# Mamba block in a four-layer graph network: the engines' order written out, one slot per state

## The chip, the cores and the metric

The kernel runs on one core of a Trainium2 chip. The metric is the device time in microseconds of one execution; the median of three runs of the kernel before is 3628.54 us (3626.14 to 3638.55). A core has five engines that each take their instructions strictly in the order in which they were built: TensorE (PE, with its weight loads as PEld), VectorE (DVE), ScalarE (ACT), GpSimd (POOL) and SyncE (SP), which here only issues DMAs. An instruction that must wait holds back everything behind it on its engine.

## The reference

There are 3327 nodes with 256 features and a 3327 x 3327 weighted adjacency. Four layers follow each other, each of the form `x = layernorm(x + layer(x, adj))`. The change touches layer 1, a graph convolution followed by a Mamba block (float32):

```python
h = relu(adj @ x @ gcn_w + gcn_b); h = layernorm(h) * ln_g + ln_b
xz = h @ w_in; xc, z = xz[:, :512], xz[:, 512:]
u = silu(causal_conv4(xc) + conv_b)
dbc = u @ w_xp                           # 16 step-size ranks, 16 of B, 16 of C
dt = softplus(dbc[:, :16] @ w_dt + b_dt)
dA = exp(dt[:, :, None] * A);  dBu = dt * B * u
hst = dA_t * hst + dBu_t;  ys_t = hst @ C_t      # scan over the 3327 rows
y = (ys + u * D_skip) * silu(z);  out = y @ w_out
```

The scan runs along the nodes, for each of 512 channels and each of 16 states.

## The kernel before

The nodes are padded to 26 tiles of 128. Layer 0 comes first, then the Mamba stage, then the graph attention of layer 2 and the two-step attention of layer 3. Work is traced in the text through a scheduling layer, which builds each engine's order and the semaphores from the data flow; the order of the text is a priority, not a rule. `issue_after` and `keep_in_program_order` fix an instruction behind another one of its engine.

In the Mamba stage the nodes lie along the free axis, in chunks of at most four tiles (512 columns), and the 512 channels lie on the partitions in four groups (NG = 4). The chunks have 2, 2, 3, 4, 4, 4, 4, 3 tiles. For each chunk the loop runs over 16 states; (chunk, state) is one step of the main loop, called a slot in this document. A slot has

- four decays on ACT (`decay`, L255 by its helper): `dA = exp(dt * A)` into one of two PSUM tiles;
- a feed on POOL (`feed`, L498): `h = du * B`, for the slot two later, into one of two tiles `h`;
- four scans on DVE (`scan`, L259 by its helper), each over one channel group, with the last column of the chunk before as its start (`carry`, copied by ACT in L587);
- the product with C on DVE (`product`, into one of two tiles `hc`), which the PE transposes and adds up into PSUM tiles `y`, one per node tile (`add_up`, L519).

Around this recurrence lies work that is spread over the slots. `convolve` is a generator of the graph convolution for one tile after the other (26 matmuls of 128x256 in groups of JM = 6, L278; a copy `m`, two transposes, a copy, the product with `gcn_w`, a Relu; then `measure`, `norm` and `turn`, which are statistics on DVE and POOL, a normalization on ACT and two transposes into `hT`). `pace` advances it so that it stays ahead of the chunks. `head(c + 1)` prepares the next chunk from slot 3 of chunk c, one step a slot: four input projections with the convolution's taps (to slot 8), Silu, the product with `w_xp` (slot 9), two step sizes in slot 10 and two in slot 11 (L437 to L440 on PE and ACT, then L445 on ACT), the subtraction of the softplus on DVE and Ln on ACT in slot 12, and the rest in slots 13 and 14. `gate_input` computes z in slots 2 to 5, and its Silu is in slot 8 of the text. `back(c - 1)` finishes the chunk before: gate, transposes and the output projection with the residual in slot 0, the normalization in slot 4. `values` is layer 2's value computation for finished tiles, two steps a slot once the convolution is done.

Two chains fix part of the order: `chained` queues scans, products, taps and the head's DVE steps in the order of the text, and `decaying` does so for the decays, the Silu calls and Ln on ACT. The rest of each engine's order is the scheduler's choice.

PSUM has eight banks: four `y`, two `dA`, one `cb` for the convolution, and one `ps` that projections, step sizes, `turn`, `gate_input`, `back` and `values` all share.

Of the kernel before, what the change touches and what calls it, by code (L numbers as in the profile page):

```python
# [9 lines left out]
F32 = mybir.dt.float32  # L10
# [15 lines left out]
NS = 6  # L26
# [19 lines left out]
def gnn_kernel(ctx: ExitStack, tc: tile.TileContext, n: int, a: dict, out: bass.AP):  # L46
# [109 lines left out]
    with tc.tile_pool(name="l1b", bufs=1) as wpool, tc.tile_pool(name="l1at", bufs=2) as l1at:  # L156
# [33 lines left out]
        with tc.tile_pool(name="l1aw", bufs=1) as cwork, tc.tile_pool(name="l1c", bufs=2) as ch, \  # L190
                tc.tile_pool(name="l1t", bufs=3) as tmp, tc.tile_pool(name="l1s", bufs=2) as work, \
# [53 lines left out]
            while not ends or ends[-1] < npad:  # L245
                prev = ends[-1] if ends else 0
                ends.append(min(npad, prev + min(WC, max(2, len(ends) + 1) * P)))
# [3 lines left out]
            chain, decays = [], []  # L251

            def decaying(*x, **k):
                with tc.issue_after(decays[-1].ins) if decays else nullcontext():
                    decays.append(nc.scalar.activation(*x, **k))  # L255

            def chained(op, *x, **k):
                with tc.issue_after(chain[-1].ins) if chain else nullcontext():
                    chain.append(op(*x, **k))  # L259

            def power(rs, var):

                nc.gpsimd.tensor_scalar(rs, var, EPS, None, op0=ALU.add)
                nc.gpsimd.tensor_tensor(rs, rs, mhalf[:, :var.shape[1]], op=ALU.pow)

            def convolve():
# [3 lines left out]
                for it in range(nt):  # L270
                    cb = cpsum.tile([P, 2, D], F32, name="cb")
                    acc, tp = cb[:, 0, :], cb[:, 1, :]
                    for j in range(nt):
# [4 lines left out]
                        nc.tensor.matmul(acc, at[:, j % JC, :], X0[:, j, :], start=(j == 0), stop=(j == nt - 1))  # L278
# [5 lines left out]
                    nc.scalar.copy(m, acc)  # L284
# [5 lines left out]
                    for k in range(2):  # L290
                        nc.tensor.transpose(tp[:, k * P:(k + 1) * P], m[:, k * P:(k + 1) * P], ident)
                    mt = cwork.tile([P, D], F32, name="m")
                    nc.scalar.copy(mt, tp)
                    for k in range(2):
                        nc.tensor.matmul(acc, mt[:, k * P:(k + 1) * P], gw[:, k, :], start=(k == 0), stop=False)
                    nc.tensor.matmul(acc, one, gb, start=False, stop=True)
                    h = cwork.tile([P, D], F32, name="hn")
                    nc.scalar.activation(h, acc, AF.Relu)  # L298
# [4 lines left out]
                    def measure(h=h, rs=rs, nb=nb):  # L303
                        mv = small.tile([P, 2], F32, name="mv")
                        stats(mv, h)
                        power(rs, mv[:, 1:2])
                        nc.gpsimd.tensor_scalar(nb, mv[:, 0:1], rs, -1.0, op0=ALU.mult, op1=ALU.mult)

                    def norm(h=h, rs=rs, nb=nb):
                        tc.keep_in_program_order(nc.scalar.activation(h, h, AF.Identity, scale=rs, bias=nb))  # L310

                    def turn(it=it, h=h):
                        c = next(x for x in range(nch) if it * P < ends[x])
                        i = it * P - starts[c]
                        if i == 0:
                            hTs[c] = ch.tile([P, D // P, WC], F32, name="hT")
                        pt = psum.tile([P, WC], F32, name="ps")
                        for k in range(2):
                            nc.tensor.transpose(pt[:, k * P:(k + 1) * P], h[:, k * P:(k + 1) * P], ident)
                        for k in range(2):  # L320
                            nc.scalar.activation(hTs[c][:, k, i:i + P], pt[:, k * P:(k + 1) * P], AF.Identity,
                                                 scale=g1[:, k:k + 1], bias=b1[:, k:k + 1])
                    rest = [lambda: None, measure, lambda: None, norm, turn]
# [4 lines left out]
                for step in rest:  # L328
# [21 lines left out]
            def pace(c, s):  # L350


                c, s = divmod(c * DS + s + DS - 3, DS)
                t0 = ends[c] if c < nch else npad
                t1 = ends[c + 1] if c + 1 < nch else npad + P
                target = NS * (t0 + (t1 - t0) * (s + 1) / DS) / P + NS - 1
                while taken < target:
                    if not advance():
                        for _ in range(2):
                            values()  # L360
                        return

            def value(it):

                pt = psum.tile([P, WC], F32, name="ps")
                for k in range(2):
                    nc.tensor.transpose(pt[:, k * P:(k + 1) * P], X[:, it, k * P:(k + 1) * P], ident)
                xt = cwork.tile([P, D], F32, name="m")
                nc.scalar.copy(xt, pt[:, :D])
                yield  # L370
                po = psum.tile([P, WC], F32, name="ps")
                for k in range(2):
                    nc.tensor.matmul(po[:, :D + 2], xt[:, k * P:(k + 1) * P], wg[:, k, :], start=(k == 0), stop=(k == 1))
                nc.scalar.copy(col[:, it, :], po[:, D:D + 2])
                g = F[:, it, D:]
                nc.scalar.activation(g, col[:, it, 0:1], AF.Exp, scale=0.2)
                nc.scalar.mul(F[:, it, :D], po[:, :D], g)
# [12 lines left out]
            def project(c, g, w):  # L390
                ps = psum.tile([P, WC], F32, name="ps")
                for k in range(2):
                    nc.tensor.matmul(ps[:, :w], w_in[:, k, g * P:(g + 1) * P], hTs[c][:, k, :w],
                                     start=(k == 0), stop=(k == 1))
                return ps[:, :w]

            def head(c):

                w = ends[c] - starts[c]
                xc = scratch()
                nc.gpsimd.tensor_copy(xc[:, :, :3], last)
                u = us[c] = ch.tile([P, NG, WC], F32, name="u", bufs=1)[:, :, :w]
                for g in range(NG + 2):
                    if g < NG:
                        nc.scalar.copy(xc[:, g, 3:3 + w], project(c, g, w))
# [1028 lines left out]
```

## Time and profile before

| what | value |
|---|---|
| median of three runs | 3628.54 us (3626.14 to 3638.55) |
| the profiled execution | 3631.34 us, its span 3629.5 us |
| mean granted clock | 0.957 |
| PE, DVE, ACT, POOL busy over the span | 3275.3, 2412.7, 1709.0, 937.9 us |
| first scan to last product of the Mamba stage | 442.2 to 1473.3 us |
| a scan of 512 columns | 1264 ns, 256 of them |
| a product of 2048 columns | 2288 ns, 64 of them |
| a decay of 512 columns | 689 ns, 256 of them |
| a feed of 2048 columns | 4530 ns, 64 of them |
| an ACT table load | 1283 ns, 32 in the stage |

The profile is one execution taken by the hardware profiler. Busy time is the time in which an engine executed; the idle time ahead of an instruction is put down to what released it. A line of the form `DVE t L259 <- ACT t L445: 39.8, 6, 12.4` says that DVE's instruction that writes tile `t` in line 259 waited for ACT's instruction that writes `t` in line 445, 39.8 us in all, 6 times, 12.4 us at most. In a timeline, a row gives start, length, engine, line, operation, output and inputs, and in brackets the idle time ahead of it. Durations of neighbouring instructions on DVE and ACT overlap by some tens of ns, so a run of four is shorter than four times one. Because operations go through helpers, scans, products and taps share L259 and are told apart by their tiles.

### The profile page before, as it was taken

To read this page: it belongs to the slowest core of one execution; us is meant where nothing else is said; L and a number is where in the kernel's file an instruction comes from. 1 tells how busy PE (TensorE), PEld (TensorE's weight loads), DVE (VectorE), ACT (ScalarE), POOL (GpSimd) and SP (SyncE) were. 2 spreads that over 40 slices of the span, in tenths; PEclk is the share of its full clock that TensorE was granted. 3 is DMA by queue.
4 is the path that set the end of the run, shared out by engine and by line. 5 is a ranking of instruction groups with operands and counts; after the bars stand their busy time and mean duration, and the time that the engine had idled before them with its cause. 6 is when DMAs were issued, how large, how long until landed. Compare 5 with 4: busy or idle time off the path is not lost. (4 is left out here: it accounts for less than half of the span.)

```text
span 3629.5 us, 43459 instructions
## 1 busy us (share of the span) xinstructions
PE 3275.3 (90%) x15583; PEld 2562.6 (71%) x15583; DVE 2412.7 (66%) x5460; ACT 1709.0 (47%) x2642; POOL 937.9 (26%) x967
## 2 busy tenths in 40 slices
PE   9999988888788666699979999999999899999996
PEld 7888666666665445588858777787777667777775
DVE  1111287888989988677753445445451999999996
ACT  1000466556555565211133333333335888888883
POOL 0000154555555545111110000000000233333332
PEclk9999999998999888799989999999999999999998
DMA  7443334333333222244422121121222122222220
GB/s 249 135 140 99 104 100 108 102 95 110 96 103 88 60 53 57 90 138 147 147 63 63 47 66 56 54 65 51 60 63 64 47 62 63 68 68 68 68 60 19
DMA packets 151996, 308.01 MB, mean 85 GB/s; under 512 B 19858, under 2 KB 77394, under 8 KB 151634
## 3 DMA queue, kind: packets, MB, share of 16 engines
q1 hardware_dynamic: 151762, 305.06, 28.4%
q8 instruction: 126, 2.06, 0.2%
q14 instruction: 108, 0.88, 0.1%
HBM read 294.36 MB, written 10.65 MB: 84 GB/s over the span
## 5 line engine op out<-in xcount | busy, mean ns | idle before, releaser
L498 POOL TENSOR_TENSOR h<-du,row 128x2048 f32<-128x2048 f32 (+2 forms) x128 | 475.6, 3716 | 411.4 <-DVE hc L259 310.3
L259 DVE TENSOR_TENSOR_SCAN h<-dA,carry,h 128x512 f32<-128x512 f32 (+2 forms) x448 | 478.8, 1113 | 54.3 <-ACT dA L255 51.3
L255 ACT ACTIVATE dA<-dt,A_log 128x512 f32<-128x512 f32 (+2 forms) x512 | 309.0, 609 | 232.0 <-DVE h L259 228.0
L912 PE MATMUL acc<-X,wt 128*128 128x256 f32 x1352 | 345.2, 392 | 10.5 <-ACT wt L910 10.2
L879 PE MATMUL acc<-F,at 128*128 128x256 f32 x1352 | 352.4, 386 | 1.0 <-ACT q L653 0.6
L278 PE MATMUL cb<-F,at 128*128 128x256 f32 x1352 | 333.6, 397 | 12.2 <-ACT hn L298 12.1
L912 PE MATMUL acc<-G,wt 128*128 128x256 f32 x1352 | 336.0, 391 | 4.4 <-ACT wt L843 4.0
L519 PE MATMUL y<-ident,hc 128*128 128x128 f32 x1664 | 249.4, 302 | 77.7 <-DVE hc L259 77.4
L912 PEld LDWEIGHTS acc<-X,wt 128*128 128x128 f32 x1352 | 243.7, 190 | 105.7 <-issue 41.3
L118 PE MATMUL acc<-xa,at 128*128 128x257 f32 x1352 | 308.4, 381 | 6.0 <-DMA at<-in_adjT 6.0
L278 PEld LDWEIGHTS cb<-F,at 128*128 128x128 f32 x1352 | 263.6, 200 | 69.2 <-ACT hn L298 18.2
L519 PEld LDWEIGHTS y<-ident,hc 128*128 128x128 f32 x1664 | 217.2, 157 | 130.9 <-DVE hc L259 100.0
L879 PE MATMUL acc<-X,at 128*128 128x256 f32 x1352 | 308.4, 381 | 0.0
L788 PE MATMUL acc<-F,at 128*128 128x257 f32 x1352 | 304.5, 381 | 1.7 <-DMA U<-in_U 1.7
L912 PEld LDWEIGHTS acc<-G,wt 128*128 128x128 f32 x1352 | 249.9, 192 | 63.9 <-ACT wt L843 33.8
L924 DVE MAX8 cand<-e 128x8 f32<-128x128 f32 x676 | 142.2, 279 | 227.7 <-ACT e L865 216.2
L879 PEld LDWEIGHTS acc<-F,at 128*128 128x128 f32 x1352 | 237.1, 190 | 74.9 <-issue 50.2
L118 PEld LDWEIGHTS acc<-xa,at 128*128 128x128 f32 x1352 | 255.2, 190 | 43.2 <-issue 6.7
L879 PEld LDWEIGHTS acc<-X,at 128*128 128x128 f32 x1352 | 252.9, 191 | 39.8 <-issue 6.6
L788 PEld LDWEIGHTS acc<-F,at 128*128 128x128 f32 x1352 | 254.1, 191 | 37.6 <-issue 1.9
L259 DVE TENSOR_TENSOR hc<-h,row 128x2048 f32<-128x2048 f32 (+2 forms) x128 | 246.5, 1926 | 4.7
L910 ACT COPY wt<-tp 128x512 f32<-128x512 f32 (+1 forms) x182 | 93.8, 557 | 310.8 <-PE tp L908 310.3
(302 smaller groups left out, 5180.3 us busy)
## 6 DMA issues: line engine op xcount, KB each, us to landing
at<-in_adjT SPq DMA_DIRECT2D x102, 832.0 KB, 4.5
at<-in_adjT SPq DMA_DIRECT2D x260, 320.0 KB, 3.0
row<-bc SPq DMA_DIRECT2D x64, 512.0 KB, 4.9
at<-in_adjT SPq DMA_DIRECT2D x52, 576.0 KB, 4.1
at<-in_adjT SPq DMA_DIRECT2D x26, 512.0 KB, 3.7
row<-bc SPq DMA_DIRECT2D x32, 384.0 KB, 4.8
row<-bc SPq DMA_DIRECT2D x32, 256.0 KB, 4.6
xt<-in_xT SPq DMA_DIRECT2D x26, 128.0 KB, 4.1
```

Source lines behind the costliest of these rows:

```text
L118: nc.tensor.matmul(acc, at[:, j, :], rhs[:, j0 + j, :], start=(j0 + j == 0), stop=(j0 + j == nt - 1))
L255: decays.append(nc.scalar.activation(*x, **k))
L259: chain.append(op(*x, **k))
L278: nc.tensor.matmul(acc, at[:, j % JC, :], X0[:, j, :], start=(j == 0), stop=(j == nt - 1))
L498: nc.gpsimd.tensor_tensor(hs[k % 2][:, :, :w], du, rows[k][:, 0:1, :].to_broadcast([P, NG, w]), op=ALU.mult)
L519: nc.tensor.matmul(y[:, g * P:(g + 1) * P], h[:, g, i * P:(i + 1) * P], ident, is_transpose=True, start=(first and g == 0), stop=(last and ...
L788: nc.tensor.matmul(acc, at[:, j, :], F[:, j0 + j, :], start=(j0 + j == 0), stop=(j0 + j == nt - 1))
L879: nc.tensor.matmul(acc, at[:, j, :], rhs[:, j0 + j, :], start=(j0 + j == 0), stop=(j0 + j == nt - 1))
L910: copy(wt[:, :m, :], pt[:, :m, :])
L912: nc.tensor.matmul(acc, wt[:, j, :], rhs[:, j0 + j, :], start=(j0 + j == 0), stop=(j0 + j == nt - 1))
L924: nc.vector.max(cand[:, s * 8:(s + 1) * 8], z[:, s * SEG:(s + 1) * SEG])
```

## The change

In the main loop of the Mamba stage every instruction on PE, DVE, ACT and POOL is now pinned behind the one traced before it on its engine (`Ordered`, `pinned`), so each engine's order is the order of the text; DMAs stay free. The text is written in slots:

- A slot begins with the `add_up` of the slot before, then four scans with the decays, the carry, the product and the feed.
- The next chunk's head is a class `Head` with one method for each step, called in fixed slots: projections in 5 and 6, taps in 7 to 9, Silu in 9 (with that of z), `mixed` in 10, step sizes in 10, 11, 11 and 12, the exponentials in 12, the subtraction and Ln in 13, `finish` in 14, `skip` in 15. The four Exp and the four Identity of 128x512 become one each of 128x2048. The step size stays in the scratch tile.
- The chunk before is finished tile by tile: gates in slot 0 between the scans, transposes and projection of one tile in each of slots 1 to 4, its residual add on DVE in the slot after, its statistics one slot later, the scales in slot 6, the normalization in 7 and 8. z is computed in 7 and 8.
- `uses` are a slot's pieces that go through `ps`; the convolution's steps (`work_ahead`, in number by `quota`) are put between and behind them. The convolution has one more yield a tile (NS = 7), and its lead begins at slot 5 (S0).
- `value` goes through the bank `cb` instead of `ps`; the scratch pool has four buffers instead of three, and `hT` three instead of two.
- The chunks have 2, 2, 3, 3, 4, 4, 4, 4 tiles.

```diff
-NS = 6
+NS = 7
+S0 = 5
...
-                ends.append(min(npad, prev + min(WC, max(2, len(ends) + 1) * P)))
+                ends.append(min(npad, prev + min(WC, (2 + len(ends) // 2) * P)))
...
+                def __getattr__(self, name):
+                    op = getattr(self.engine, name)
+                    if not pinned:
+                        return op
+                    return lambda *x, **k: tc.keep_in_program_order(op(*x, **k))
+            ten, vec, act, gps = (Ordered(x) for x in (nc.tensor, nc.vector, nc.scalar, nc.gpsimd))
...
-                    rest = [lambda: None, measure, lambda: None, norm, turn]
+                    rest = [lambda: None, measure, lambda: None, lambda: None, norm, turn]
...
-                pt = psum.tile([P, WC], F32, name="ps")
+                pt = cpsum.tile([P, WC], F32, name="cb")
...
+                def step_size(self, g):
+                    w = self.w
+                    if g == 0:
+                        self.v, self.e = (scratch()[:, :, :w] for _ in range(2))
+                    ps = psum.tile([P, WC], F32, name="ps")
+                    k = slice(32 * g, 32 * g + DTR)
+                    ten.matmul(ps[:, :w], w_dt[k, :P], self.left[k], start=True, stop=True)
+                    act.activation(self.v[:, g, :], ps[:, :w], AF.Identity, bias=b_dt[:, g:g + 1])
+                    act.activation(self.e[:, g, :], ps[:, :w], AF.Abs, bias=b_dt[:, g:g + 1])
+                def exponentials(self):
+                    e = self.e
+                    act.activation(e, e, AF.Exp, scale=-1.0)
+                    self.e1 = scratch()[:, :, :self.w]
+                    act.activation(self.e1, e, AF.Identity, bias=1.0)
+                def logarithms(self):
+                    vec.scalar_tensor_tensor(self.e, self.e1, 1.0, self.e, op0=ALU.subtract, op1=ALU.subtract)
+                    act.activation(self.e1, self.e1, AF.Ln)
...
+                if added:
+                    add_up(*added)
                 for g in range(NG):
                     scan(k, g, dAs.pop(0))
...
+                    if c and s == 0:
+                        for i in range(tiles_of(c - 1)):
+                            if min(i + 1, NG - 1) == g:
+                                gate(c - 1, i)
+                    if g == 0 and s - 1 in sums:
+                        sums.pop(s - 1)()
+                    if g == 1 and c and 2 <= s < 2 + tiles_of(c - 1):
+                        measured(plus["mv"][:, s - 2, :], X[:, starts[c - 1] // P + s - 2, :])
+                act.copy(carry[:, s, :], hs[k % 2][:, :, w - 1])
...
+                if s == 9:
+                    act.activation(szs[c], szs[c], AF.Silu)
+                if after:
+                    for g in {7: (0, 1), 8: (2,), 9: (3,)}.get(s, ()):
+                        ahead.taps(g)
+                    if s == 9:
+                        ahead.silu()
+                    elif s == 13:
+                        ahead.logarithms()
+                    elif s == 14:
+                        ahead.finish()
+                added = ys[c], product(k), False, s == DS - 1
...
+                if after:
+                    if s in (5, 6):
+                        if s == S0:
+                            pump(ends[c + 1] // P)
+                        uses += [lambda g=g: ahead.project(g) for g in (2 * s - 10, 2 * s - 9)]
+                    if s == 10:
+                        uses += [ahead.mixed]
+                    uses += [lambda g=g: ahead.step_size(g) for g in {10: (0,), 11: (1, 2), 12: (3,)}.get(s, ())]
+                    if s == 12:
+                        uses += [ahead.exponentials]
+                    if s == 15:
+                        uses += [ahead.skip]
...
+                q = quota(c, s) if done < nt else 2
+                for use in uses[:1]:
+                    use()
+                work_ahead((q + 1) // 2)
+                for use in uses[1:]:
+                    use()
+                work_ahead(q // 2)
```

## The prediction

> **What bounds the kernel now.** I read the page's busy shares first, then the busy time by stage, then VectorE's waits in the stage that the diff touches, then its timeline in one chunk. Over the whole span PE is busiest, but the edit is confined to the Mamba stage, from 440 to 1475 us, so that stage is read alone. The columns are length, then busy us (instructions) of PE, PEld, DVE, ACT, POOL, then clock, DMA share and GB/s.
>
> ```profile
> span 3629.5 us, 43459 instructions
> 440.00:1475.00 1035.00, 807.75 (x3837) 601.43 (x3836) 895.96 (x889) 611.26 (x1196) 552.78 (x235) 0.90 0.33 88
> ```
>
> DVE is busy 896 of 1035 us, more than PE (808), so DVE bounds the stage and its idle time is what an order can win. VectorE's waits from 438 to 1475 us (total, times, longest):
>
> ```profile
> DVE h L259 <- ACT dA L255: 55.9, 43, 4.2
> DVE t L259 <- ACT t L445: 39.8, 6, 12.4
> DVE bnst L86 <- ACT hn L298: 25.6, 6, 10.6
> DVE u L259 <- ACT u L408: 3.1, 2, 1.7
> ```
>
> With four small ones (2.6, 2.5, 1.4, 0.9) this is 131.8 us, the most that a perfect order could save. I laid the waits on the 128 states (a "slot": four scans and a product) by the products' times. Slot 12 of each chunk holds 63 us (4.6, 11.0, 14.1, 10.0, 12.6, 3.3, 6.8, 0.2 in chunks 0 to 7), slot 9 holds 23, all others 46. Chunk 4 shows both kinds, an undisturbed slot and slot 12 (DVE's timeline, then ACT's beside it):
>
> ```profile
> 1010.20 4.80 DVE L259 TENSOR_TENSOR_SCAN h<-dA,carry,h 128x512 f32<-128x512 f32 x4
> 1015.09 2.29 DVE L259 TENSOR_TENSOR hc<-h,row 128x2048 f32<-128x2048 f32 x1
> 1017.30 4.80 DVE L259 TENSOR_TENSOR_SCAN h<-dA,carry,h 128x512 f32<-128x512 f32 x4
> ...
> 1041.89 2.29 DVE L259 SCALAR_TENSOR_TENSOR t<-t 128x2048 f32<-128x2048 f32 x1 [12.41 <-ACT t L445]
> ```
> ```profile
> 1026.34 0.67 ACT L438 ACTIVATE t<-ps,b_dt 128x512 f32<-128x512 f32 x1
> 1026.91 0.68 ACT L439 ACTIVATE t<-ps,b_dt 128x512 f32<-128x512 f32 x1
> ...
> 1029.75 0.69 ACT L438 ACTIVATE t<-ps,b_dt 128x512 f32<-128x512 f32 x1 [1.03 <-PE ps L437]
> ...
> 1040.20 1.66 ACT L445 ACTIVATE t<-t 128x512 f32<-128x512 f32 x3
> 1041.76 0.38 ACT L298 ACTIVATE hn<-cb 128x256 f32<-128x256 f32 x1
> 1042.15 1.28 ACT L255 ACT_TABLE_LOAD   x1
> ```
>
> A full slot takes 7.1 us (1010.20 to 1017.30). In slot 12, DVE stands before the subtraction of the softplus until ACT has worked off 14 us of step-size work, which comes one slot before its consumer.
>
> **The change part by part.** No engine gains work worth a term: the built programs differ by 48 ACT instructions fewer (and three tiny POOL ones more), and after the Mamba block the order on all five engines is the same. What moves is the order in the block.
>
> *Slot 12.* The head starts at slot 5 instead of 3, its step sizes lie in slots 10, 11, 11, 12, the joined exponentials in 12, the subtraction in 13. What is late next is found from ACT's room. Counted from the start of a full slot, the fourth scan ends at 4.8; a decay (0.6) and the carry (0.2) follow, so other ACT work starts at 5.6 and must end by 8.8, for the third decay (0.7) to be there at 7.1 + 2.4 = 9.5. That is room for 3.2 us. Slot 10 has the 112-row copy and one pair, 0.5 + 1.2: it fits. Slot 11 has two pairs with a PE round trip between (1.2 + 0.9 + 1.2), then a conv tile's copy, norm and two turned copies (0.3 + 0.5 + 0.7), which again wait for PE: about 2.2 over. Slot 12 has a pair and two 2048-wide activations (1.2 + 0.3 + 1.9 + 1.9): 2.1 over. Slot 13 has a table load, Ln and a load (1.28 + 1.9 + 1.28) after the subtraction, against 4.8 less a decay: 1.0 over. So 5.3 a head at full width; the narrow heads' shorter slots take most of what their shorter work gives, and I take 4.5 for seven heads, 31 us. Saved: 63 - 31 = 32.
>
> *Slot 9.* Both Silu calls stay there (load 1.28, 1.9, 1.9, load 1.28, with a Relu 0.4 between), now with one tap group (2.2) before the product, so 6.7 against 3.2 + 2.2: 1.3 over at full width, some 2 on the narrow slots. Eight chunks at 1.6 are 13. Saved: 23 - 13 = 10.
>
> *The other slots.* The skip product with a conv tile's copies (slot 15) is 1.3 over. A finished tile of the chunk before is now projected a slot at a time, and DVE adds it after the next slot's first scan. If the conv's turn stands before it in PE's fixed order, that add waits some 2 us, which is new. With the two projection slots I take 4.5 a chunk, 36 in all, against 46. Saved: 10.
>
> *PE's fixed order.* PE goes through one PSUM tile `ps` for nearly all helpers, and a second use in a slot must wait until ACT has copied the first (about 6 us into the slot). Behind the waiting matmul stand the conv steps and the next slot's transposes; product k waits for the transposes of k-2, so a slot of lateness is covered, but ACT's copies wait for PE, and the decays stand behind them. No row shows this wait in a fixed order. From below it is nothing, as PE has 227 us of idle time here; from above, 1.0 us a slot, as long as the round trip in the row at 1029.75, 128 us. I take 10, near the low end, because that round trip comes at most twice a slot and usually inside ACT's room; both ends go to the range.
>
> The Trainium skill, in "Perfetto Trace Analysis", Identifying the Most-Contended Engine, says that matmul busy time misjudges PE and the weight loads' share should be read instead; here that is 601 of 1035 us (58%) against 78%. By that share the term would be nearer 0; the sum keeps 10.
>
> *Joined activations.* Four Exp and four Identity of 512 become one each: three pieces took 1.66, so four take 2.2, and one of 2048 elements 1.9. That is 0.6 a head on ACT, inside the slot-12 figure. The skill's section Optimizing Scalar/DVE Operations, on the same page, says that breaking instructions up may help where ACT is not saturated but makes bubbles elsewhere, which speaks against joining. If a joined call held a decay back by its extra 1.4 us, eight heads would lose 2 x 1.4 x 8 = 22 us; the rows leave these calls in slot 12 behind both early decays in either form, so I book no such loss.
>
> *Chunks 2, 2, 3, 3, 4, 4, 4, 4.* The same widths in another order, so DVE's sum is unchanged. In PE's built order, the conv tiles done beside chunks 1 and 2 fall from 3.8 and 4.4 to 3.0 and 4.0, so the lead stays covered (7.0 tiles after chunk 0, 7.5 before). The tail has four tiles to finish rather than three: a tile's period is 3.9 us (1479.78 to 1483.68). The value step now uses the bank `cb`, which lets it lie beside the residuals (before, the third residual came 7.3 after the second). I take +2, between 0 and +4.
>
> *The first head.* Before, from 420 to 433.5 us ACT mixed conv work into the first step sizes; now four pairs, one Exp and one Identity follow each other, some 10.5 us instead of 13.5: -3, between 0 and -5.
>
> *The rest.* Row and adjacency DMAs are the same in number and on the same SP queue; the B/C rows are written in slot 10 and first read in slot 14, four slots (28 us) against a landing time of 4.9. The feeds on POOL still follow the product and take 4.5 of 7.1 us. The fourth scratch buffer and the step size in place cost nothing.
>
> The waits become 31 + 13 + 36 + 10 = 90 instead of 131.8, so -42; with +2 and -3 the sum is -43. The profiled execution took 3631.3 us (its span 3629.5), 2.8 above the median of the runs; -43 from the median, 3628.5, gives 3585.5, and I say 3586.
>
> **The rivals.**
> *A: ping-pong on `ps` and `cb` decides (slower).* Place: the second use in a slot and the copies behind it on ACT, ahead of the decays. For it: PE is 78% busy, the slots of 256 columns last only 3.7 us, and a round trip (1 us) does not shrink with them. Against: 227 us of PE idle. It decides from 0.33 us a slot more than I booked (43/128); at the upper end, 128 instead of 10, the time is 3628.5 - 43 + 118 = 3704; at half of that excess, 3645.
> *B: the stalls only move.* The 42 us that went from slots 9 and 12 come back in slots 4, 11 and 15. For it: ACT is full in those slots by the sum above. Time: 3628 - 1, about 3627.
> *C: nearly all waits go.* If PE's lateness is nothing and the overruns of slots 11 to 13 are hidden by DVE's own extra work (some 24 us a full chunk beyond its 16 slots of 7.1), the 13 and 36 remain: 3628.5 - 83 - 1 = 3545.
> *D: the change does nothing*, since each engine already ran a fixed order: excluded as such, as the orders differ throughout the block.
>
> **How the numbers follow.** Mine 0.50, C 0.17, B 0.12, A 0.21. The range reaches from just above C's figure to just below A's half: 3550 to 3640, with about a tenth left out at each end; my case alone runs from 3560 (PE's term nothing, half of the overruns hidden) to 3612 (PE's term 36). About 0.3% (11 us) is what a measurement tells from no change. Faster is mine and C with a hundredth of B, 0.68. Within it are 0.10 of B and 0.02 of A, 0.12. Slower is the rest, 0.20.
>
> **What would show it.** Right: the wait of `t` on the joined Identity falls from 40 us to under 10, DVE's waits in the block to 70 to 110, no slot is above 16 us, and DVE's busy time stays near 896. Wrong: a new wait of the X add on `ps`, or of `dA` behind copies in every slot, above 60 us together; a block longer than 1035 us; or PE waiting for ACT in most slots.

## The result, and the profile after

The changed kernel takes 3740.84 us (median of 4 runs, 3739.81 to 3741.57) against 3630.73 us before (median of 4, 3626.14 to 3638.55): a ratio of 1.0301 with a 95% interval of 1.0282 to 1.0320, 110 us slower. The forecast was 3586, its range 3550 to 3640: wrong in sign and outside the range. Of the experiments below, pin_pe and pin_pool each had one run in a slower state, which is left out of their figures.

The span of the profiled execution, and the busy time in the Mamba stage of the kernel after (columns as in the view by stage shown for the kernel before):

```profile
span 3739.6 us, 43358 instructions
433.00:1590.00 1157.00, 852.84 (x3853) 654.07 (x3853) 900.54 (x886) 606.64 (x1150) 519.71 (x239) 0.84 0.29 79
```

DVE is as busy as before (901 us, 896 before), but the stage is longer: from the first scan to the last product it takes 1156.5 us (433.3 to 1589.8), 125 more than the 1031.1 before. Around it 13 us are gained: the first scan comes 9 us earlier, and from the last product to layer 2's first `w` 28.3 us pass instead of 32.6. So the loss is idle time of DVE in the block. Laid on the slots by the products' times it is 247.9 us, against 130.8 before (each with 2.5 us ahead of the first scan):

| slot | 0 | 1 | 2 | 3 | 4 | 5 | 6 | 7 | 8 | 9 | 10 | 11 | 12 | 13 | 14 | 15 |
|---|---|---|---|---|---|---|---|---|---|---|---|---|---|---|---|---|
| before, us | 2.7 | 0 | 0 | 4.7 | 13.5 | 7.4 | 2.2 | 0.5 | 1.4 | 22.9 | 0.5 | 2.5 | 62.6 | 5.5 | 3.8 | 0.6 |
| after, us | 9.0 | 5.8 | 12.5 | 17.9 | 14.3 | 2.0 | 35.6 | 31.0 | 11.4 | 7.0 | 19.7 | 28.9 | 23.3 | 17.1 | 12.4 | 0 |

The peak of slot 12 is gone, and nearly every other slot has a wait. To read the second row: most of what the text puts into a slot on PE and ACT stands behind that slot's product, so its lateness shows at the third scan of the next slot. The projections written in slots 5 and 6 show in columns 6 and 7, the Silu calls of slot 9 in column 10, the steps from `mixed` to Ln (slots 10 to 13) in columns 11 to 14. The last chunk, which prepares no head, has no wait at all in columns 6, 7 and 11 to 14.

VectorE's waits and ScalarE's waits of the kernel after in this stage (total, times, longest):

```profile
DVE h L263 <- ACT dA L263: 201.0, 74, 7.2
DVE X L263 <- PE ps L263: 28.4, 18, 3.4
```
```profile
ACT t L263 <- PE ps L263: 87.1, 41, 5.1
ACT col L263 <- PE cb L263: 40.0, 19, 4.4
...
ACT u L263 <- POOL t L263: 31.4, 7, 5.9
```

DVE waits for decays 201 us (55.9 before) and no longer for the softplus (39.8 before). ScalarE is no busier than before (607 us, 611 before); what it gained is waiting: all its waits for PE in the stage add up to 225 us, against 94 before.

The timeline of the kernel after in chunk 4, slots 5 and 6, ScalarE first, then GpSimd, TensorE and VectorE, shows two ways in which this reaches DVE:

```profile
991.23 0.58 ACT L263 COPY t<-ps 128x512 f32<-128x512 f32 x1
997.66 0.81 ACT L263 ACTIVATE u<-t,conv_b,conv_w 128x512 f32<-128x512 f32 x1 [5.86 <-POOL t L263]
...
999.97 1.28 ACT L263 ACTIVATE dA<-t,A_log 128x512 f32<-128x512 f32 x2
...
1006.84 0.59 ACT L263 COPY t<-ps 128x512 f32<-128x512 f32 x1 [2.86 <-PE ps L263]
...
1011.16 0.58 ACT L263 COPY t<-ps 128x512 f32<-128x512 f32 x1 [2.88 <-PE ps L263]
1011.78 0.81 ACT L263 ACTIVATE u<-t,conv_b,conv_w 128x512 f32<-128x512 f32 x1
1012.50 1.28 ACT L263 ACTIVATE dA<-t,A_log 128x512 f32<-128x512 f32 x2
```
```profile
992.99 4.50 POOL L263 TENSOR_TENSOR h<-du,row 128x2048 f32<-128x2048 f32 x1 [2.58 <-DVE hc L263]
997.43 0.20 POOL L263 COPY t<-last 128x12 f32<-128x12 f32 x1
```
```profile
1004.92 1.88 PE L263 MATMUL ps<-hT,w_in 128*128 128x512 f32 x4
1006.64 2.76 PE L263 MATMUL cb<-F,at 128*128 128x256 f32 x12
1009.24 1.88 PE L263 MATMUL ps<-hT,w_in 128*128 128x512 f32 x4
```
```profile
1000.68 2.46 DVE L263 TENSOR_TENSOR_SCAN h<-dA,carry,h 128x512 f32<-128x512 f32 x2 [5.45 <-ACT dA L263]
...
1013.20 2.46 DVE L263 TENSOR_TENSOR_SCAN h<-dA,carry,h 128x512 f32<-128x512 f32 x2 [4.77 <-ACT dA L263]
```

In slot 5 ScalarE's convolution `u` needs the three halo columns that GpSimd copies; the copy takes 0.20 us but stands behind a feed of 4.5 us, and the third and fourth decay of the next slot stand behind `u`. In slot 6 ScalarE waits at two copies for the projections, between which PE has twelve convolution matmuls, and again the decays stand behind. Slot 10 of the same chunk shows the second way where little work is written: the copy of `mixed` and the first pair of step sizes take 1.85 us together, but wait 8.1 us for PE, and VectorE waits 6.1 us (ScalarE, then VectorE):

```profile
1053.30 0.58 ACT L263 COPY t<-ps 112x512 f32<-112x512 f32 x1 [5.01 <-PE ps L263]
1056.95 1.27 ACT L263 ACTIVATE t<-ps,b_dt 128x512 f32<-128x512 f32 x2 [3.06 <-PE ps L263]
1058.10 1.30 ACT L263 ACTIVATE dA<-t,A_log 128x512 f32<-128x512 f32 x2
```
```profile
1058.83 2.46 DVE L263 TENSOR_TENSOR_SCAN h<-dA,carry,h 128x512 f32<-128x512 f32 x2 [6.09 <-ACT dA L263]
```

### The profile page after: what moved, and what is told of

It reads as the page before. It is cut to its first block, busy times and chain, and to the rows that moved or that the text cites. A ratio compares the mean times of both kernels' runs of the same rounds, so it can differ in the third digit from the quotient of the medians.

```text
span 3739.6 us, 43358 instructions
## 1 busy us (share of the span) xinstructions
PE 3301.6 (88%) x15583; PEld 2604.1 (70%) x15583; DVE 2418.5 (65%) x5460; ACT 1705.0 (46%) x2594; POOL 903.5 (24%) x970
## 5 line engine op out<-in xcount | busy, mean ns | idle before, releaser
L263 ACT ACTIVATE dA<-t,A_log 128x512 f32<-128x512 f32 (+2 forms) x510 | 305.3, 609 | 276.8 <-DVE h L263 274.3
L263 PE MATMUL cb<-F,at 128*128 128x256 f32 x1148 | 296.4, 411 | 69.4 <-ACT hn L263 69.1
L263 PEld LDWEIGHTS cb<-F,at 128*128 128x128 f32 x1148 | 232.3, 207 | 133.0 <-ACT hn L263 77.2
L263 PEld LDWEIGHTS y<-ident,hc 128*128 128x128 f32 x1648 | 231.4, 166 | 110.1 <-DVE hc L263 97.1
L995 PE MATMUL tp<-ident,e 128*128 128x128 f32 x1352 | 196.6, 277 | 43.1 <-DVE e L1182 35.1
```

The lines of the kernel that those rows point to most:

```text
L263: return lambda *x, **k: tc.keep_in_program_order(op(*x, **k))
L995: nc.tensor.transpose(pt[:, j, :], e[:, (j0 + j) * P:(j0 + j + 1) * P], ident)
```

## The experiments

All kernels here compute the whole reference. Each ratio is against runs of the kernel before on the same chip, each time a median of at least 4 runs.

### Two waits inside the written order

**halo_early**: the kernel after, with the halo's copy ahead of slot 5's feed on GpSimd.

```diff
+                def halo(self):
+                    self.xc = scratch()
+                    gps.tensor_copy(self.xc[:, :, :3], last)
...
+                if s == S0 and after:
+                    ahead.halo()
                 added = ys[c], product(k), False, s == DS - 1
```

> Part done differently: in slot 5 the three-column halo copy on POOL (0.2 us) is put ahead of that slot's feed (4.5 us) instead of behind it. Theory H (the POOL order costs by itself): ACT's wait for POOL in the projections, 31.4 us in 7 waits, goes, and with it DVE's idle time at slot 6, 35.6 us; time 3741 - 31 to 36, about 3707. Rival P (PE's fixed order stands ready to take its place: the convolution waits for the same Relu and the second projection comes late anyway): under 10 us are won, 3731 or more.

Measured: 3711.83 us, ratio 1.0218 (1.0199 to 1.0237), 29 us less than the kernel after. DVE's idle time in the block falls by 31 to 217.1 us, in slot 6 from 35.6 to 14.4 and in slot 7 from 31.0 to 21. ScalarE's waits for GpSimd fall from 35 to 4 us. So the halo explains 29 us, and not more, in the pinned kernel.

**uses_first**: the kernel after, with all pieces on `ps` of a slot ahead of the convolution's steps.

```diff
-                for use in uses[:1]:
+                for use in uses:
                     use()
-                work_ahead((q + 1) // 2)
-                for use in uses[1:]:
-                    use()
-                work_ahead(q // 2)
+                work_ahead(q)
```

> Part done differently: a slot's convolution steps all stand behind its pieces that use the shared PSUM tile, none between them. Theory P (a conv group of 2.8 us on PE between two uses holds ACT, and behind it the decays): slots 6, 10, 11 lose about 2.8 us each in seven chunks, some 55 us in all, time about 3685, and ACT's waits for PE fall from 224 to about 150 us. Rival Q (PE is simply late, whatever stands between): the same lateness reaches the first use of the next slot, time within 15 us of 3741.

Measured: 3806.8 us, ratio 1.0476 (1.0457 to 1.0495), 66 us more than the kernel after; DVE idles 298.1 us. Neither theory's figure is met. PE itself now waits longer for ScalarE between two uses (34.8 us for `t` and 45.9 us for `gt`, in the kernel after 6.6 and 28.9). The convolution between the uses is not what delays them as a whole; it fills a wait that is there anyway.

### The slots without the pins, the chunks alone

**slots_unpinned**: the text, slots and chunks of the kernel after, but only the two chains of the kernel before (scans, products and head steps on DVE; decays, Silu and Ln on ScalarE), and, as there, the priority of the carry and the fixed place of the convolution's norm.

```diff
-            pinned = True
+            pinned = False
...
+            vecq, actq = Queued(nc.vector, chain), Queued(nc.scalar, decays)
...
-                vec.tensor_tensor_scan(h, dA, h, ...
+                vecq.tensor_tensor_scan(h, dA, h, ...
...
-                act.activation(dA, dt[:, g, :], AF.Exp, ...
+                actq.activation(dA, dt[:, g, :], AF.Exp, ...
```

> Part undone: the text with its slots and its chunk lengths stays, but only what was chained before is chained (scans, products, taps and the head's steps on DVE; decays, Silu and Ln on ACT); PE, POOL and the rest of ACT and DVE are left to the scheduler again. Theory P (the pins are the loss, the slots are sound): DVE's slot-12 wait goes without the new waits, 3590 to 3630. Rival T (the slots of the text are the loss): 3700 or more.

**old_chunks**: the kernel after with 2, 2, 3, 4, 4, 4, 4, 3 tiles.

```diff
-                ends.append(min(npad, prev + min(WC, (2 + len(ends) // 2) * P)))
+                ends.append(min(npad, prev + min(WC, max(2, len(ends) + 1) * P)))
```

> Part undone: chunks of 2, 2, 3, 4, 4, 4, 4, 3 tiles again, the pinned order stays. If the chunk lengths cost nothing, as the prediction has it: 3730 to 3750. Rival C (the last chunk's longer slots or the longer tail cost): 3725 or less.

Measured: slots_unpinned 3601.44 us, ratio 0.9913 (0.9891 to 0.9936); old_chunks 3740.1 us, ratio 1.0298 (1.0279 to 1.0317). The chunks cost nothing. The slots by themselves gain 29 us on the kernel before, and the pins cost 139 us on top of them. In slots_unpinned DVE idles 111.9 us in the block, 52.3 of it in slot 13. VectorE's timeline there in chunk 4, and ScalarE's beside it:

```profile
982.47 4.80 DVE L278 TENSOR_TENSOR_SCAN h<-dA,carry,h 128x512 f32<-128x512 f32 x4
994.40 0.43 DVE L285 BATCH_NORM_STATS2 bnst<-hn 128x6 f32<-128x256 f32 x1 [7.13 <-ACT hn L326]
...
996.21 2.31 DVE L278 SCALAR_TENSOR_TENSOR t<-t 128x2048 f32<-128x2048 f32 x1 [1.16 <-ACT t L480]
```
```profile
991.48 0.68 ACT L473 ACTIVATE t<-ps,b_dt 128x512 f32<-128x512 f32 x1
992.19 1.91 ACT L478 ACTIVATE t<-t 128x2048 f32<-128x2048 f32 x1
994.01 0.36 ACT L326 ACTIVATE hn<-cb 128x256 f32<-128x256 f32 x1
994.27 1.90 ACT L480 ACTIVATE t<-t 128x2048 f32<-128x2048 f32 x1
```

The statistics wait is put down to a Relu, but that Relu stands between the two halves of a step size that comes too late: the old stall of slot 12, one slot further on.

### Which engine's order costs what

**pin_pe, pin_act, pin_dve, pin_pool**: slots_unpinned with the order of one engine pinned (here ScalarE).

```diff
+            FIXED = (nc.scalar,)
...
-                    if not pinned:
+                    if not pinned or self.engine not in FIXED:
                         return op
...
-            pinned = False
+            pinned = True
```

> From the version with only the old chains (slots_unpinned, 3601 us), PE alone is pinned to the text's order. Theory P (PE's fixed order makes the ping-pong): most of the 139 us come back, 3690 or more. Rival A (ACT's fixed order does it, since the decays stand behind copies that wait for PE): under 3640.

> From the version with only the old chains (3601 us), ACT alone is pinned to the text's order. Theory A (the decays stand behind copies that wait for PE and POOL): 3670 or more, and the wait for the halo copy on POOL, some 30 us, shows again only if POOL's own order puts it behind the feed. Theory P: under 3640. If both this and the run with PE pinned stay under 3640, only the two together cost.

> From the version with only the old chains (3601 us), DVE alone is pinned to the text's order: statistics, residual adds and gates stand where the text has them. By the trace of slots_unpinned 47 us of its DVE waits are statistics that stand too early, before the softplus subtraction; if the text's place for them is better, some 30 us are won: 3570 to 3585. Rival (residual adds wait for PE, 28 us in the changed kernel): 3601 to 3635.

> From the version with only the old chains (3601 us), POOL alone is pinned to the text's order. Theory H (the halo copy behind the feed holds ACT's projection): about 30 us more, 3625 to 3640. Rival (with the decays free to pass ahead of the waiting activation, nothing is lost): 3595 to 3610.

**free_act, free_pe**: the kernel after with one engine freed. free_act leaves PE, DVE and POOL pinned (`FIXED = (nc.tensor, nc.vector, nc.gpsimd)`) and gives ScalarE the old chain (with the carry's priority and the norm's place, as in slots_unpinned); free_pe has one line.

```diff
             pinned = True
+            ten = nc.tensor
```

> The kernel after with one engine's order given back: ScalarE follows dependencies again, with only the old chain of its decays, Silus and logarithms, while TensorE, VectorE and GpSimd keep the order of the text. If the lost time is ScalarE's decays standing behind copies that wait for TensorE and GpSimd (theory A, order on ScalarE), the decays pass the waiting copies: 60 to 75 us come back and 3665 to 3680 us are left, the remainder being TensorE's own order, and VectorE's wait for decays in the block falls from 201 us to below 100. If TensorE's order alone made the loss (rival), nothing much comes back: above 3715 us, with VectorE's 201 us for decays kept.

> The kernel after with TensorE alone freed to follow dependencies, the other three engines in the order of the text. If TensorE's fixed order feeds ScalarE's copies late and the decays wait behind them (the term of the prediction), most of the 139 us come back: below 3670 us, with VectorE's wait for decays below 100 us. If ScalarE's own order is enough, as pinning it alone suggests (94 of 139 us), 15 to 45 us come back: 3695 to 3725 us, with over 150 us of waits for decays kept.

| kernel | time, us | ratio to before, 95% interval | DVE idle in the block, us | ScalarE's waits for PE, us |
|---|---|---|---|---|
| slots_unpinned | 3601.44 | 0.9913 (0.9891 to 0.9936) | 111.9 | 84 |
| pin_pe | 3663.5 | 1.0091 (1.0060 to 1.0122) | 169.9 | 106 |
| pin_act | 3695.48 | 1.0184 (1.0147 to 1.0220) | 196.9 | 239 |
| pin_dve | 3614.92 | 0.9959 (0.9945 to 0.9973) | 120.0 | 84 |
| pin_pool | 3599.17 | 0.9910 (0.9880 to 0.9939) | 111.4 | 74 |
| after (all four) | 3740.84 | 1.0301 (1.0282 to 1.0320) | 247.9 | 225 |
| free_act (three) | 3658.57 | 1.0077 (1.0055 to 1.0100) | 162.4 | 104 |
| free_pe (three) | 3730.29 | 1.0265 (1.0247 to 1.0284) | 233.1 | 204 |

ScalarE's order is the largest part both ways: 94 us when it is pinned alone, 82 us back when it alone is freed. In pin_act VectorE's wait for decays is nearly that of the kernel after (43.9 us in slots_unpinned):

```profile
DVE h L280 <- ACT dA L265: 175.9, 73, 8.9
```

TensorE's costs 62 us alone, between the two theories' figures, by waits of another kind (VectorE waits 42.2 us for `y` and 49.8 us for the softplus, decays stay at 38.2), but freeing it in the pinned kernel returns only some 13 us by the ratios (0.0036 of 3631): below the 15 to 45 expected, and its decays stay late (VectorE's waits of free_pe):

```profile
DVE h L263 <- ACT dA L263: 198.5, 75, 8.9
```

VectorE's order costs 13.5 us, where a gain was expected: the wait of the statistics only turned into the softplus's own (47.9 us). GpSimd's costs nothing alone.

With PE free and ScalarE pinned (pin_act) ScalarE's waits for PE are as long as with both pinned (239 and 225 us); with ScalarE free and PE pinned they are 104 (free_act) and 106 (pin_pe). So it is ScalarE's own queue that makes it stand before copies whose matmuls have not run yet. What it does when it is free is seen in free_act, chunk 4, on ScalarE's timeline, at two copies of z:

```profile
989.65 0.59 ACT L513 COPY sz<-ps 128x512 f32<-128x512 f32 x1 [3.87 <-PE ps L265]
990.13 0.70 ACT L280 ACTIVATE dA<-t,A_log 128x512 f32<-128x512 f32 x1
...
993.46 0.69 ACT L280 ACTIVATE dA<-t,A_log 128x512 f32<-128x512 f32 x1
994.22 0.20 ACT L653 COPY carry<-h 128x4 f32<-128x4 f32 x1
...
996.22 0.58 ACT L513 COPY sz<-ps 128x512 f32<-128x512 f32 x1 [1.21 <-PE ps L265]
```

Decays and the carry are built between the copies, where the text has them before or after. What free_act has left is VectorE's waits

```profile
DVE h L265 <- ACT dA L280: 58.0, 32, 6.6
DVE t L265 <- ACT t L482: 56.9, 6, 12.8
```

that is, decays as before the change, and the softplus wait again, now in slot 13 (58.7 us of idle time there). The pins had held it back only by making the slots ahead of it longer; this last is an inference, no run isolates it.

**halo_free**: free_act with the halo's copy ahead of the feed, the edit of halo_early.

> The kernel with ScalarE's order given back (free_act, 3659 us) and the halo's copy on GpSimd ahead of the feed. If the halo cost 29 us in the fully pinned kernel only because decays stood behind ScalarE's waiting convolution, which they can now pass, nothing is left to win: 3652 to 3664 us. If the late convolution itself holds the head up, 15 to 29 us go here too: 3630 to 3644 us.

Measured: 3654.17 us, ratio 1.0069 (1.0052 to 1.0085), 3 us less than free_act by the ratios (4 by the medians), inside the intervals. So the halo's 29 us and ScalarE's 82 us are not two causes: the late convolution holds up the head by nothing that counts; it costs because decays are queued behind it.

### Is it the single buffer?

The prediction's rival A named the one buffer of `ps` and of `cb`. Two pairs of kernels give a second buffer. In the first the decays' tiles move to SBUF, which frees two banks.

```diff
-                tc.tile_pool(name="l1a", bufs=2, space=PSUM) as apsum, \
+                tc.tile_pool(name="l1a", bufs=2) as apsum, \
```

> The kernel after with the decays' two tiles in SBUF instead of PSUM, nothing else: the control for the next run. The scans then read both inputs from SBUF. If the place of the decays is of no account, 3735 to 3746 us; if ScalarE's writes or VectorE's reads there are slower, more, which the next run then shares. DVE's scan of 1.2 us each tells it.

**da_sbuf_two** adds `bufs=2` for the pools of `ps` and `cb`.

> As the control, with the two banks that became free given to `ps` and `cb` as second buffers: TensorE can go on to a helper's second use before ScalarE has copied the first. If the ping-pong on single buffers holds the pinned copies up (rival A of the prediction), at least 50 of the 139 us that the pins cost come back against the control: 3690 us or less with a control of 3741, and ScalarE's waits for `ps` and `cb`, some 224 us in the kernel after, fall by half. If the copies simply stand too early in ScalarE's order, whatever the buffers, less than 20 us come back: 3721 us or more.

Measured: da_sbuf 3980.81 us, ratio 1.0966 (1.0947 to 1.0984); da_sbuf_two 3943.97 us, ratio 1.0863 (1.0839 to 1.0888). The second buffers return 37 us, between the two theories' figures, and the control is no longer the same kernel: it is 240 us slower than the kernel after, for a reason given in the last section. ScalarE's waits for PE fall from 215 to 138 us, by less than half. The pair is inconclusive. The second pair keeps the decays in PSUM and has chunks of at most three tiles, so that one accumulator's bank is free.

```diff
-                ends.append(min(npad, prev + min(WC, (2 + len(ends) // 2) * P)))
+                ends.append(min(npad, prev + (3 if ends else 2) * P))
...
-                tc.tile_pool(name="l1p", bufs=1, space=PSUM) as psum, \
+                tc.tile_pool(name="l1p", bufs=2, space=PSUM) as psum, \
```

The first line alone is **threes**, both are **threes_ps2**.

> The kernel after with chunks of 2, 3, 3, 3, 3, 3, 3, 3, 3 tiles: the control for the next run. One chunk more is 16 more slots of VectorE's fixed cost (a slot of four tiles takes 7.1 us, one of three 5.5), about 16 x 0.7 = 11 us, and shorter slots leave ScalarE less room for the same copies: 3770 to 3830 us by both theories.

> As the control, with the free bank as a second buffer of `ps`. If the ping-pong on the single `ps` makes ScalarE's copies late and the decays behind them (the prediction's rival A), at least 30 us less than the control, and ScalarE's waits for `ps` (some 145 us in the kernel after) fall by half or more. If the buffer is not what holds them (order alone), within 10 us of the control.

Measured: threes 3755.86 us, ratio 1.0328 (1.0311 to 1.0345), less than was expected of the control; threes_ps2 3731.8 us, ratio 1.0262 (1.0245 to 1.0279): 24 us, again between the figures. VectorE's waits tell what they are, first threes, then threes_ps2:

```profile
DVE h L263 <- ACT dA L263: 169.6, 70, 16.8
DVE X L263 <- PE ps L263: 69.9, 23, 4.7
```
```profile
DVE h L263 <- ACT dA L263: 170.0, 69, 16.5
DVE X L263 <- PE ps L263: 42.6, 23, 2.4
```

The wait for decays does not move at all; what falls is the wait of the residual add for its projected tile, by 27 us. ScalarE's waits for PE fall from 180 to 159 us, not by half. The single buffer of `ps` has a price, but it is not what holds the decays. A second `cb` beside decays in PSUM was not run, so its share stays open.

### The slot-12 stall without pins

**early_head**: slots_unpinned with the next chunk's head one slot earlier, the subtraction left in slot 13.

```diff
-S0 = 5
+S0 = 4
...
-                    uses += [lambda g=g: ahead.step_size(g) for g in {10: (0,), 11: (1, 2), 12: (3,)}.get(s, ())]
-                    if s == 12:
+                    uses += [lambda g=g: ahead.step_size(g) for g in {9: (0,), 10: (1, 2), 11: (3,)}.get(s, ())]
+                    if s == 11:
                         uses += [ahead.exponentials]
```

(Projections, taps, Silu, `mixed` and `gate_input` move by one slot likewise.)

> The kernel with the slots of after and only the old chains (3601 us), with the whole head of the next chunk one slot earlier: projections in slots 4 and 5, step sizes in 9 to 11, softplus subtraction still in 13. If VectorE's 52 us of waits in slot 13, 47 of them the norm's statistics standing behind the joined Exp, are step-size work that comes too late (theory L), they go: 3555 to 3575 us, slot 13 below 10 us. If the waits belong to the place of the norm among ScalarE's work wherever the step sizes stand (rival), slot 13 keeps over 30 us: 3590 to 3605 us.

**split_exp**: slots_unpinned with Exp and Identity one per group again.

```diff
+                    act.activation(self.e[:, g, :], self.e[:, g, :], AF.Exp, scale=-1.0)
...
-                    act.activation(e, e, AF.Exp, scale=-1.0)
...
-                    act.activation(self.e1, e, AF.Identity, bias=1.0)
+                    for g in range(NG):
+                        act.activation(self.e1[:, g, :], e[:, g, :], AF.Identity, bias=1.0)
```

> The kernel with the slots of after and only the old chains (3601 us), with the softplus's Exp and Identity again one instruction per group of 128 channels, as in the kernel before. If the joined pair of 1.9 us each makes the wait in slot 13 (theory J: the whole of it falls in one slot and the norm's Relu and copies stand behind it), 10 to 20 us go: 3580 to 3592 us. If only the lateness of the last step sizes counts, the same within 5 us: 3596 to 3606 us. If joining really saves time, slower by up to 10 us.

**b_slot**: the kernel before, its head begun at state 2 and an empty step between the step sizes and the subtraction.

```diff
-                if 3 <= s < DS - 1 and c + 1 < nch:
-                    if s == 3:
+                if 2 <= s < DS - 1 and c + 1 < nch:
+                    if s == 2:
...
+                yield None
```

(`pace` is told of the earlier start in two places.)

> The kernel before, its planner and its chains kept, with the head of the next chunk begun one state earlier and one empty step between the step sizes and the softplus subtraction. If the 63 us in slot 12 are the subtraction standing a slot too close to its last step size and nothing else (theory S), most of them go and no order has to be pinned for it: 3575 to 3590 us. If the wait passes to what comes next on the same engines, as slot 13 did in the unpinned slots (rival), 20 to 30 us go at most: 3600 to 3612 us.

Measured: early_head 3582.2 us, ratio 0.9857 (0.9839 to 0.9875); split_exp 3611.24 us, ratio 0.9944 (0.9928 to 0.9961); b_slot 3594.41 us, ratio 0.9888 (0.9863 to 0.9913). In early_head slot 13 falls from 52.3 to 18.8 us, and VectorE's waits are now mostly for decays (the whole block):

```profile
DVE h L278 <- ACT dA L278: 55.0, 48, 3.4
```

The direction is the first theory's, the size is not: 19 us are gained rather than 26 to 46. Of the 33.5 us that slot 13 loses, 12 come back beside it (slot 12 goes from 1.1 to 7.5 us, slot 14 from 3.6 to 9.1), and the column in which both Silu calls show, now 9, keeps its wait (26.5 us, against 23.2 in column 10 of slots_unpinned). In b_slot slot 12 falls from 62.6 to 25.5 us; the 37 us gained lie between the two theories' figures, nearer to the first: the stall can be halved and more without any pin, and a rest stays. Breaking the joined calls up did not help; it is some 10 us slower by the medians (3611 and 3601, on two chips; the intervals of the ratios touch), so joining cost nothing in these slots.

## Why the prediction was wrong

- **DVE bounds the stage and its idle time is the prize: right.** DVE's busy time stayed (896 and 901 us), and the loss is idle time, 130.8 to 247.9 us.
- **Slot 12: right in mechanism, too low in what follows it.** The softplus wait is gone from the pinned slots, as predicted. But the head's steps that the prediction sums up in slots 10 to 13 make VectorE wait 81.7 us (columns 11 to 14), not 31. The sum of ScalarE's room had the durations of its instructions in it, and of waits for PE little more than one round trip of 0.9 us in slot 11. Slot 10 "fits" by that sum; it measures 28.9 us, with waits of 5.0 and 3.1 us for PE in chunk 4. (The terms given for slot 13, 4.46 against 4.1 us, make 0.4 over and not 1.0; that is small beside the rest.)
- **Slot 9: right in mechanism, too low.** The Silu calls written in slot 9 show in column 10: 19.7 us where 13 were booked. Of the 22.9 us before, 3 are saved and not 10. The 7.0 us in column 9 are not theirs.
- **The other slots: wrong by 110 us**, 100 if the 10 of PE's order are counted here. 36 were booked, the remaining columns measure 146.5 us. 66.6 us of it lie in columns 6 and 7, behind the projections, where the two projection slots had 4.5 us a chunk together with the skip product and the residual add. The residual add's wait, foreseen as new, is 28.4 us. "The feeds on POOL still follow the product and take 4.5 of 7.1 us" is true, and was booked at nothing; but the halo's copy waits behind a feed, ScalarE waits for the copy, and the decays wait for ScalarE (29 us, by halo_early).
- **PE's fixed order: the step that failed.** It was bounded by 0 and 128 us and taken at 10, since a round trip of 1 us comes "at most twice a slot and usually inside ACT's room". The sentence "ACT's copies wait for PE, and the decays stand behind them" describes what happened; but the price was put on PE's order and on the buffer, and ScalarE's pin had no term of its own. Measured, ScalarE's order is worth 82 us; PE's is worth 13 once ScalarE is pinned and 62 when it is pinned alone, so that 10 was too low even for the engine that was named. And the round trip is not 1 us: behind twelve convolution matmuls the copies wait 2.9 us each, in a queue with four decays a slot behind them.
- **Joined activations, chunks: right.** No loss by joining (split_exp, in the unpinned slots), none by the chunks (old_chunks). The first head gained 9 us, not 3; the tail gained 4 instead of losing 2.
- **The rivals.** A was the right side, at its upper end and beyond (3704 forecast, 3741 measured), with the wrong agent: a second `ps` returns 24 us and none of the wait for decays, though the share of `cb` was not measured. B holds in part, for the unpinned slots, where the stall moved to slot 13. C fell. The signs named as "wrong" (a wait of `dA` behind copies above 60 us, a block longer than 1035 us) are what the profile after shows.

The prediction's sum without the term for PE's order would be -53 us; the same slots without the pins gave -29. So the new places by themselves are worth about half of what the sum gave, with 52.3 us of idle time left in slot 13, and the pins turned the gain into a loss.

## What to carry to other kernels

In these runs an instruction that only copies a result out of PSUM cost the decays little more than its duration in a free queue, and its duration plus the producer's lateness in a pinned one: when an order is written out by hand, price each queue by what its instructions wait for, and look first at what critical work (here the decays) stands behind a waiting one. Pinning must pay by itself: test the new places of the work with the old freedom, because here the places gained 29 to 49 us (slots_unpinned, early_head) and the pins cost 139. A consumer that stands a slot too close to its producer can be helped by the distance alone: b_slot, which starts the head of the kernel before one state earlier and puts one step between, gains 1.1% (0.9888); early_head, the fastest of all, gains 1.4%.

## What the runs showed of the hardware

**A scan with two inputs in SBUF stands still while GpSimd works on SBUF.** In da_sbuf the 512-column scan takes 2216 ns in the mean instead of 1268. VectorE's and GpSimd's timelines of da_sbuf:

```profile
1117.58 2.46 DVE L263 TENSOR_TENSOR_SCAN h<-dA,carry,h 128x512 f32<-128x512 f32 x2 [1.62 <-ACT dA L263]
...
1126.62 9.02 DVE L263 TENSOR_TENSOR_SCAN h<-dA,carry,h 128x512 f32<-128x512 f32 x4
```
```profile
1117.65 1.58 POOL L263 TENSOR_TENSOR rs<-rs,mhalf 128x1 f32<-128x1 f32 x1
...
1126.84 5.37 POOL L263 TENSOR_TENSOR h<-du,row 128x2048 f32<-128x2048 f32 x1 [6.73 <-ACT sz L263]
```

Four scans beside a feed take 9.02 us instead of 4.80, so 4.2 us more, about one feed (4.53 us in the kernel before), and two scans without a feed beside them take their usual 2.46. The first scan was under way when the feed began; behind the feed's end (1132.21) the other three, 3.6 us long, would end at 1135.8, and the run of four ends at 1135.64. GpSimd is held up in turn: the feed takes 5.37 us, and the power of one column beside the two scans 1.58 us, where it took 0.57 in the kernel after with VectorE idle (at 1012.56 us). With the decays in PSUM, in the kernel after, two scans ran from 992.77 to 995.22 inside a feed (992.99 to 997.49) at 2.45 us. So it is the decays' place in PSUM that lets the feeds lie beside the scans, and moving them cost 240 us. The Trainium skill, "SBUF — State Buffer", Who interferes with whom, says that a VectorE instruction with two SBUF inputs contends with a GpSimd instruction that reads SBUF. The table in its section Summary: rules for kernel authors adds that the second one to issue fully blocks until the first finishes. These rows agree.

**The same matmuls ran slower in the longer stage.** PE's busy time in the stage rose from 807.75 to 852.84 us with practically the same instructions (3837 and 3853), as the granted clock fell from 0.90 to 0.84. In early_head, whose stage is shorter, the clock is 0.90 again. How much of the copies' longer waits for PE comes from this no run separates, so it is not counted as a cause.
